# A third product split into quarters, and a reordered value stage, in a cross-attention kernel

## The chip, the core and the metric

The kernel runs on one core of a Trainium2 chip. The metric is the device time of one execution in microseconds (us). Three executions of the kernel before gave 2172.95, 2173.05 and 2175.15 us; the median is 2173.05 us.

## The reference, cut to what matters

The program is a block of three layers on 128 latent tokens of width 512: a double attention (one on the latents themselves, one on a context of 12544 tokens), a causal self-attention, and a mixture of 32 experts. Nearly all of the time goes to the attention on the context:

```python
kvx = jnp.einsum('bsi,oi->bso', cond, w_kv_x)          # 12544 x 512 times 512 x 2048
kx, vx = jnp.split(kvx, 2, axis=-1)
kx = _ln(kx.reshape(b, sc, g, d), kxln_w, kxln_b)      # 8 groups of 128
vx = vx.reshape(b, sc, g, d)
xout = _gqa(qx, kx, vx).reshape(b, s, nh * d)          # 16 heads, two to a group
```

All of it is in fp32.

## The kernel before

**Chunks.** The context is cut into 25 chunks of 512 tokens; the middle one (chunk 12) has 256. For each chunk TensorE makes keys (`KT`, transposed, 8 groups) and values (`V`), then the scores of every group (`s_ps`, function `scores`) and the weighted values (`o_ps`, function `outputs`). Softmax is done with a running maximum: `max_rows` and `spread` find and spread the shift, `weigh` takes the exponential on ScalarE, rescales the running output `ol` by `al`, and adds the probabilities into the running sum on GpSimd.

**Seven products instead of eight.** Keys and values of a chunk are each a product of a 512-wide contraction. It is made as a two by two block product with seven block products (numbered 0 to 6 in the lists `mixed_w` and `mixed`), of sums of the weights (`wsum`, made once) and sums of the tokens (`mix_tokens`, on GpSimd, for each chunk). For whole chunks (`whole(c)`: all but chunk 0 and chunk 12; 23 of them) products 1 and 3 are themselves made from seven quarter products each. That is what `fine` does in `k_chunk` and `v_chunk`, with token sums from `mix_finer_tokens` and weight sums from `mix_finer_weights`. The other five products use `mm`.

**Banks.** All of these products go through the pool `ps_kv` of three PSUM banks. A bank is filled, read by an add on VectorE or a copy on ScalarE, and filled on: several products accumulate in one bank (`a`), and between two of them its contents have to be read. A matmul that writes a bank therefore waits for the reading instruction before it.

**Order of the work.** `v_chunk` is a generator. The loop over the eight groups of a chunk issues `scores(c, g)`, then one step of `v_chunk`, then `maxima`. After the scores, `keys(c + 1, ...)` steps `k_chunk` for the next chunk, and after each step `others(i)` issues `outputs(c, i)`. So the values of chunk c are made between its scores, and the keys of chunk c + 1 between its outputs. The tile framework turns this into one order for each engine, in which an instruction may move a little, and sets the semaphores. Every engine then runs its own list in order.

At the boundary, the last thing in `v_chunk` is product 6 into bank `a`, then two adds on VectorE (L593 and L594). Then `k_chunk` opens three banks:

```python
b, a, d = bank("fb_ps"), bank("fa_ps"), bank("fc_ps")
fine(b, 1, True)
fine(a, 0, True)
p1 = kept(a, "p1", groups)
add(to(0, 0), groups(b), p1)
fine(d, 4, True)
```

`kept` is a copy on ScalarE into a `u` buffer, of which there are two. `fc_ps` gets the bank that L594 reads last.

**Squares of the keys.** `k_sums` squares four groups of keys on ScalarE, 512 columns at a time, into one buffer `sq`, and VectorE reduces each (L603 and L604). `k_rstd` makes the scale `krs` for the scores from them: a small product (`v_ps`), an add on VectorE and a power on GpSimd (L623).

**Buffers.** Probabilities `s` have eight buffers of the pool `sp`, the rescaling tile `al` two.

Of the kernel before, what the change touches and what calls it, by code (L numbers as in the profile page):

```python
# [17 lines left out]
P = 128  # L18
H = 512
# [26 lines left out]
def block_kernel(  # L46
# [359 lines left out]
    def mix_finer_weights(v, eng):  # L406
        s1, s2, s4 = (finer[0][:, v, i] for i in range(3))
        eng.tensor_tensor(s1, finer_w(v, 1, 0), finer_w(v, 1, 1), ALU.add)
        eng.tensor_tensor(s2, s1, finer_w(v, 0, 0), ALU.subtract)
        turn_finer_weights(v, eng)  # L410
        eng.tensor_tensor(s4, finer_w(v, 0, 1), s2, ALU.subtract)

# [9 lines left out]
    def mix_finer_tokens(c, eng):  # L422
        t = finp.tile([P, 2, 3, P], F32, tag="fx", name=f"finer_{c}")
        finer_x[c] = []
        for i, x in enumerate((mixed[c][1], mixed[c][3])):
            b11, b12 = x[:, 0, 0:P], x[:, 0, P : 2 * P]
            b21, b22 = x[:, 1, 0:P], x[:, 1, P : 2 * P]
            t1, t2, t4 = (t[:, i, j, :] for j in range(3))
            eng.tensor_tensor(t1, b12, b11, ALU.subtract)
            eng.tensor_tensor(t2, b22, t1, ALU.subtract)  # L430
            eng.tensor_tensor(b12, b22, b12, ALU.subtract)
            eng.tensor_tensor(t4, b21, t2, ALU.subtract)
            finer_x[c].append((b11, b21, b22, t4, t1, t2, b12))
# [14 lines left out]
    def k_chunk(c):  # L448
# [36 lines left out]
        b, a, d = bank("fb_ps"), bank("fa_ps"), bank("fc_ps")  # L485
# [3 lines left out]
        add(to(0, 0), groups(b), p1)  # L489
        fine(d, 4, True)  # L490
# [15 lines left out]
        d0 = bank("c_ps")  # L506
        mm(d0, 0, 4, True)
        nc.scalar.copy(out(0, 1, 1), pair(d0))
        mm(a0, 0, 5, False)
        u2 = kept(a0, "u2", pair)  # L510
        yield
        mm(d0, 0, 2, False)
        add(out(0, 0, 1), pair(d0), u2)
        mm(a0, 0, 6, False)
        add(out(0, 1, 1), pair(a0), out(0, 1, 1))
        add(out(0, 1, 0), pair(a0), out(0, 1, 0))
        a1 = bank("a_ps")
        mm(a1, 1, 0, True)
        add(out(1, 0, 0), pair(a1), out(1, 0, 0))
        yield  # L520
        d1 = bank("c_ps")
        mm(d1, 1, 4, True)
        nc.scalar.copy(out(1, 1, 1), pair(d1))
        mm(a1, 1, 5, False)
        u2 = kept(a1, "u2", pair)
        yield
        mm(d1, 1, 2, False)
        add(out(1, 0, 1), pair(d1), u2)
        yield
        mm(a1, 1, 6, False)  # L530
        add(out(1, 1, 1), pair(a1), out(1, 1, 1))
        added[0] = add(out(1, 1, 0), pair(a1), out(1, 1, 0))
        yield

    def v_chunk(c):
# [16 lines left out]
        a, b = bank("fa_ps"), bank("fb_ps")  # L552
# [3 lines left out]
        nc.vector.tensor_tensor(to(0, 0), both(b), both(p1), ALU.add)  # L556
# [3 lines left out]
        d = bank("fc_ps")  # L560
# [4 lines left out]
        nc.vector.tensor_tensor(to(1, 1), both(d), both(u3), ALU.add)  # L565
# [4 lines left out]
        nc.vector.tensor_tensor(to(0, 1), both(d), both(u2), ALU.add)  # L570
        yield
        for v in range(2):
            def mm(ps, i, first):
                w, x = mixed_w[i], mixed[c][i]
                for k in range(2):
                    last_mm[0] = nc.tensor.matmul(  # L576
                        ps, lhsT=x[:, k, v * P : (v + 1) * P], rhs=w[:, k, H : 2 * H],
                        start=first and k == 0, stop=k == 1, skip_group_check=True,
                    ).ins

            t1, t2 = V[:, v, :], V[:, 2 + v, :]
            a, d = bank("a_ps"), bank("c_ps")
            mm(a, 0, True)
            nc.vector.tensor_tensor(t1[:, :H], a, t1[:, :H], ALU.add)
            mm(d, 4, True)
            nc.scalar.copy(t2[:, H:], d)
            yield
            mm(a, 5, False)
            u2 = kept(a, "u2")
            mm(d, 2, False)  # L590
            nc.vector.tensor_tensor(t2[:, :H], d, u2, ALU.add)
            mm(a, 6, False)
            nc.vector.tensor_tensor(t2[:, H:], a, t2[:, H:], ALU.add)  # L593
            added[0] = nc.vector.tensor_tensor(t1[:, H:], a, t1[:, H:], ALU.add).ins  # L594
            yield

    def k_sums(c, u):
# [3 lines left out]
        for j in range(4):  # L601
            sq = tmpk.tile([P, CH], F32, tag="sq", name="sq", bufs=1)
            nc.scalar.activation(sq[:, :n], KT[:, 4 * u + j, :n], AF.Square)  # L603
            nc.vector.tensor_reduce(  # L604
                r[:, j, : n // 32], sq[:, :n].rearrange("p (b i) -> p b i", i=32),
                AX.X, ALU.add, apply_transpose=True,
            )
# [26 lines left out]
    def keys(c, others, pool, tag, todo=None, done=0):  # L634
# [4 lines left out]
        for i in range(done, 8):  # L639
            next(todo)  # L640
            if i in ((4, 7) if fine else (3, 7)):
                sums[i // 7] = k_sums(c, i // 7)
            if fine and i == 6:
                k_rstd(c, 0, sums.pop(0), pool, tag)
            if others:
                others(i)
            if fine:
                continue
# [872 lines left out]
```

## Time and profile before

| | us |
|---|---|
| time, three executions | 2172.95, 2173.05, 2175.15 |
| the profiled execution, its own time | 2170.52 |
| its span, first to last instruction | 2168.4 |
| TensorE busy | 2114.5 (98%) |
| VectorE busy | 1441.3 (66%) |
| ScalarE busy | 919.8 (42%) |
| GpSimd busy | 1185.6 (55%) |
| one whole chunk, from its first score product to that of the next | 76.77 |

The last row is read from the timeline of TensorE: the first score products of two following chunks start at 1151.37 and 1228.14. The other whole chunks have the same period within 0.02 us, apart from chunk 11, in front of the short one, and the last. In the profile PE is TensorE, PEld its weight loads, DVE VectorE, ACT ScalarE and POOL GpSimd. One fp32 matmul of the program is two MATMUL records. A timeline row gives the start, the length, the engine, the line, what was written from what, the shape and the number of records, and then the idle time before it with what ended it.

### The profile page before, as it was taken

To read this page: it belongs to the slowest core of one execution; us is meant where nothing else is said; L and a number is where in the kernel's file an instruction comes from. 1 tells how busy PE (TensorE), PEld (TensorE's weight loads), DVE (VectorE), ACT (ScalarE), POOL (GpSimd) and SP (SyncE) were. 2 spreads that over 40 slices of the span, in tenths; PEclk is the share of its full clock that TensorE was granted. 3 is DMA by queue.
4 is the path that set the end of the run, shared out by engine and by line. 5 is a ranking of instruction groups with operands and counts; after the bars stand their busy time and mean duration, and the time that the engine had idled before them with its cause. 6 is when DMAs were issued, how large, how long until landed. Compare 5 with 4: busy or idle time off the path is not lost.

```text
span 2168.4 us, 25820 instructions
## 1 busy us (share of the span) xinstructions
PE 2114.5 (98%) x9487; PEld 1582.4 (73%) x9487; DVE 1441.3 (66%) x2571; ACT 919.8 (42%) x1787; POOL 1185.6 (55%) x1363
## 2 busy tenths in 40 slices
PE   8999999999999999999999999999999999999999
PEld 3667877877877787787777877777787787776554
DVE  8776677677667667766777668667767766766311
ACT  3445444444535434444444445444544443541211
POOL 5245675575566557548675575566557557644000
PEclk9999999999999999999999999999999999999999
DMA  9300000000000000000000000000000000007693
GB/s 320 112 20 1 20 20 1 20 20 20 1 20 20 0 21 20 10 1 20 21 20 12 9 20 20 1 20 20 1 20 20 20 1 20 1 1 258 212 283 115
DMA packets 71230, 95.60 MB, mean 44 GB/s; under 512 B 3136, under 2 KB 39488, under 8 KB 71104
## 3 DMA queue, kind: packets, MB, share of 16 engines
q1 hardware_dynamic: 70816, 93.92, 13.4%
q8 instruction: 74, 1.21, 0.2%
q14 instruction: 52, 0.43, 0.1%
q10 hardware_dynamic: 288, 0.04, 0.0%
HBM read 93.69 MB, written 0.26 MB: 43 GB/s over the span
## 4 chain that ended last, share of the span: by engine, by line
PE 84%; DVE 9%; issue 3%; ACT 2%; POOL 1%; DMA 1%; SPq 0%; POOLq 0%; ACTq 0%; DVEq 0%
PE s_ps L925 15%; PE o_ps L1031 14%; PE a_ps L464 11%; PE a_ps L576 8%; PE c_ps L464 7%; PE c_ps L576 6%; PE gu_ps L1436 4%; PE fa_ps L541 4%; PE fa_ps L455 3%; PE fc_ps L455 2%; PE moe_acc L1457 2%; PE fc_ps L541 2%; DVE mx L953 2%; PE ps_p L722 1%; DVE mxr L936 1%
## 5 line engine op out<-in xcount | busy, mean ns | idle before, releaser
L1023 POOL TENSOR_TENSOR ol<-ol,s 128x256 f32<-128x256 f32 x764 | 550.8, 729 | 55.1 <-ACT s L1013 11.8
L1031 PE MATMUL o_ps<-s,V 128*128 128x256 f32 x1568 | 380.6, 381 | 0.9 <-DVE ol L1036 0.9
L1015 POOL TENSOR_TENSOR ol<-ol,al 128x512 f32<-128x512 f32 x192 | 242.4, 1278 | 241.1 <-DVE al L985 241.1
L930 ACT ACTIVATE s<-s_ps,krs 128x256 f32<-128x256 f32 x784 | 322.5, 472 | 119.8 <-PE s_ps L925 90.1
L925 PE MATMUL s_ps<-qxT,KT 128*128 128x256 f32 x1568 | 372.8, 381 | 0.4 <-ACT s L930 0.4
L623 POOL TENSOR_TENSOR krs<-kve,mhalf 128x16 f32<-128x16 f32 (+1 forms) x50 | 142.8, 2855 | 400.0 <-DVE kve L621 400.0
L936 DVE TRANSPOSE_TENSOR_REDUCE mxr<-s 128x32 f32<-128x1024 f32 (+1 forms) x200 | 244.2, 1221 | 162.3 <-ACT s L930 161.5
L925 PEld LDWEIGHTS s_ps<-qxT,KT 128*128 128x128 f32 x1568 | 295.8, 190 | 72.8 <-issue 35.6
L1031 PEld LDWEIGHTS o_ps<-s,V 128*128 128x128 f32 x1568 | 288.1, 190 | 36.4 <-ACT s L1013 1.3
L603 ACT ACTIVATE sq<-KT 128x512 f32<-128x512 f32 (+1 forms) x200 | 124.1, 621 | 309.1 <-DVE KT L483 216.4
L1013 ACT ACTIVATE s<-s 128x1024 f32<-128x1024 f32 (+1 forms) x200 | 201.3, 1040 | 80.3 <-DVE s L1001 80.2
L1001 DVE TENSOR_TENSOR s<-s,b_ps 128x1024 f32<-128x1024 f32 (+1 forms) x200 | 232.8, 1175 | 0.0
L1036 DVE TENSOR_TENSOR ol<-ol,o_ps 128x256 f32<-128x256 f32 x192 | 79.3, 414 | 203.1 <-PE o_ps L1031 198.4
L604 DVE TRANSPOSE_TENSOR_REDUCE sqr<-sq 128x16 f32<-128x512 f32 (+1 forms) x200 | 139.4, 697 | 72.2 <-ACT sq L603 69.4
L576 PE MATMUL a_ps<-wkv,ctx 128*128 128x512 f32 x368 | 172.9, 592 | 0.0
L464 PE MATMUL a_ps<-ctx,wkv 128*128 128x256 f32 x736 | 170.8, 380 | 0.0
L464 PEld LDWEIGHTS a_ps<-ctx,wkv 128*128 128x128 f32 x736 | 138.0, 190 | 21.4 <-DVE KT L483 3.5
L576 PEld LDWEIGHTS a_ps<-wkv,ctx 128*128 128x128 f32 x368 | 69.9, 190 | 68.4 <-issue 66.0
L445 ACT COPY u<-fa_ps 128x512 f32<-128x512 f32 x92 | 54.0, 587 | 145.2 <-PE fa_ps L455 144.2
L977 ACT ACTIVATE als<-als 128x32 f32<-128x32 f32 x48 | 11.0, 229 | 198.7 <-DVE als L976 198.7
L483 DVE TENSOR_TENSOR KT<-a_ps,KT 128x512 f32<-128x512 f32 x138 | 89.2, 673 | 6.3 <-PE a_ps L464 5.6
L1436 PE MATMUL gu_ps<-gu,xT 128*128 128x384 f32 x256 | 87.4, 486 | 0.0
(319 smaller groups left out, 3243.7 us busy)
## 6 DMA issues: line engine op xcount, KB each, us to landing
ctx<-in_ctxT SPq DMA_DIRECT2D x23, 1024.0 KB, 5.1
gu<-in_w SPq DMA_DIRECT2D x32, 384.0 KB, 4.9
gu<-in_v SPq DMA_DIRECT2D x32, 384.0 KB, 5.6
dn<-in_w SPq DMA_DIRECT2D x16, 768.0 KB, 4.9
w<-in_wprojT SPq DMA_DIRECT2D x8, 1024.0 KB, 5.8
w<-in_wqxT SPq DMA_DIRECT2D x4, 1024.0 KB, 11.3
w<-in_wqT SPq DMA_DIRECT2D x4, 1024.0 KB, 5.5
wkv<-in_wkvT SPq DMA_DIRECT2D x8, 256.0 KB, 8.2
```

What stands on the lines that cost most here:

```text
L464: nc.tensor.matmul(ps[:, j * h : (j + 1) * h], lhsT=w[:, k, (2 * u + j) * D : (2 * u + j + 1) * D], rhs=x[:, k, :], start=first and j == k ...
L576: last_mm[0] = nc.tensor.matmul(ps, lhsT=x[:, k, v * P : (v + 1) * P], rhs=w[:, k, H : 2 * H], start=first and k == 0, stop=k == 1, skip_g ...
L623: nc.gpsimd.tensor_tensor(rs[:, :, :nt], ve[:, :, :nt], mhalf.rearrange("p (g t) -> p g t", g=4)[:, :, :nt], ALU.pow,)
L925: end = nc.tensor.matmul(ps[:, t - t0, :], lhsT=KT[:, g, t * P : (t + 1) * P], rhs=qxT[:, 2 * g : 2 * g + 2, :], start=True, stop=True,)
L930: copied[0] = nc.scalar.activation(s[:, t, :], ps[:, t - t0, :], AF.Copy, scale=rs[:, t : t + 1]).ins
L936: nc.vector.tensor_reduce(mxr[g // 4][:, g % 4, :nt, :].rearrange("p t k -> p (t k)"), s[:, :nt, :].rearrange("p t (k i) -> p (t k) i", i=32),
L1001: nc.vector.tensor_tensor(s[:, :nt, :], s[:, :nt, :], ps[:, a, None, :].to_broadcast([P, nt, HS]), ALU.subtract,)
L1013: nc.scalar.activation(s[:, :nt, :], s[:, :nt, :], AF.Exp, scale=scale)
L1015: nc.gpsimd.tensor_tensor(ol[g], ol[g], rescale[j][:, a, None, :].to_broadcast([P, 2, HS]), ALU.mult)
L1023: summed[0] = nc.gpsimd.tensor_tensor(ol[g][:, 1, :], first, s[:, t, :], ALU.add).ins
L1031: end = nc.tensor.matmul(ps, lhsT=V[:, t, g * D : (g + 1) * D], rhs=s[:, t, :], start=t == 0, stop=t == nt - 1,)
L1436: nc.tensor.matmul(ps, lhsT=xT[:, k, :], rhs=experts[x][0][i][:, k], start=k == 0, stop=k == NK - 1,)
```

## The change

Four things:

- In `v_chunk`, product 2 is made from seven quarter products as well (`third`): seven matmuls of 256 columns take the place of the four of 512 columns that made product 2 for both halves. Their weight sums come from `mix_finer_weights(1, ...)` once, their token sums from `mix_third_tokens` for each chunk, both on GpSimd. Five partial results pass through a bank `t_ps`, whose two halves are filled in turn, and a bank `tb_ps`. The copies `u2` of the two `mm` halves are gone; VectorE adds bank `a` directly.
- In `k_chunk` a `yield` comes after the first two quarter products, so that all of `outputs(c, 0)` stands between them and the third one (`fc_ps`). The later steps are merged so that there are still eight.
- `k_sums` squares two groups at a time (1024 columns) and takes its buffer from the pool `sp` of the probabilities.
- `al` has one buffer, and is filled after the subtraction of the shift instead of before it. `mx4` has one buffer too. For j = 2 of a whole chunk the spreading of the shift is held back until the last add of `v_chunk`.

```diff
@@ mix_finer_weights
+        if v:
+            s1, s2, s4 = (finer[1][:, i] for i in range(3))
+            eng.tensor_tensor(s1, third_w(1, 0), third_w(1, 1), ALU.add)
+            eng.tensor_tensor(s2, s1, third_w(0, 0), ALU.subtract)
+            turn_third_weights(eng)
+            eng.tensor_tensor(s4, third_w(0, 1), s2, ALU.subtract)
...
+    def mix_third_tokens(c, eng):
+        t = finp.tile([P, 3, P], F32, tag="tx", name=f"third_{c}")
+        third_x[c] = mix_tiles(t, mixed[c][2], eng)
@@ k_chunk
-        b, a, d = bank("fb_ps"), bank("fa_ps"), bank("fc_ps")
+        b, d, a = bank("fb_ps"), bank("fc_ps"), bank("fa_ps")
         fine(b, 1, True)
         fine(a, 0, True)
         p1 = kept(a, "p1", groups)
         add(to(0, 0), groups(b), p1)
+        yield
         fine(d, 4, True)
@@ v_chunk
+        def third(ps, n, first, start=None):
+            nc.tensor.matmul(
+                ps, lhsT=tx[n], rhs=tw[n], start=first if start is None else start, stop=True,
+                skip_group_check=True,
+            )
...
+        y = bank("tb_ps")
+        third(y[:, : H // 2], 1, True)
...
+        t = bank("t_ps")
+        ta, td = t[:, : H // 2], t[:, H // 2 :]
+        third(ta, 0, True)
+        p1 = kept_half(ta, "p1")
+        add(third_to(0, 0), y[:, : H // 2], p1)
+        a = bank("a_ps")
+        mm(a, 0, 0, True)
+        add(outs(0)[0], a)
+        third(td, 4, True, False)
+        third(ta, 5, False)
+        u2 = kept_half(ta, "u2")
+        yield
+        third(ta, 6, False)
+        u3 = kept_half(ta, "u3")
+        add(third_to(1, 1), td, u3)
+        d = bank("c_ps")
+        mm(d, 0, 4, True)
+        nc.scalar.copy(outs(0)[3], d)
+        third(ta, 3, False)
+        nc.scalar.copy(third_to(1, 0), ta)
+        mm(a, 0, 5, False)
+        third(td, 2, False)
+        add(third_to(0, 1), td, u2)
+        add(outs(0)[2], d)
+        add(outs(0)[2], a)
+        yield
+        mm(a, 0, 6, False)
+        add(outs(0)[3], a)
+        add(outs(0)[1], a)
+        a = bank("a_ps")
+        mm(a, 1, 0, True)
+        add(outs(1)[0], a)
+        yield
+        d = bank("c_ps")
+        mm(a, 1, 5, False)
+        add(outs(1)[2], a)
+        mm(d, 1, 4, True)
+        nc.scalar.copy(outs(1)[3], d)
+        add(outs(1)[2], d)
+        mm(a, 1, 6, False)
+        add(outs(1)[3], a)
+        added[0] = add(outs(1)[1], a)
@@ k_sums
-        for j in range(4):
-            sq = tmpk.tile([P, CH], F32, tag="sq", name="sq", bufs=1)
+        for j in range(0, 4, 2):
+            sq = pool.tile([P, CH // P, HS], F32, tag="s", name="sq", **({} if c else {"bufs": 1}))
...
@@ spread
-        to_all(ps, sh)
-        if c:
-            rescale[j] = tmp.tile([P, 2, HS], F32, tag="al", name="al")
-            to_all(rescale[j], al)
+        with tc.issue_after(added[0]) if whole(c) and j == 2 else nullcontext():
+            to_all(ps, sh)
         for a in range(2):
...
+        if c:
+            rescale[j] = tmp.tile([P, 2, HS], F32, tag="al", name="al", bufs=1)
+            with tc.issue_after(end.ins):
+                to_all(rescale[j], al)
@@ loop over the groups
+            if g == 0 and whole(c):
+                mix_third_tokens(c, nc.gpsimd)
```

## The prediction

> **What bounds the kernel now.** I read the page's busy shares first, then the waits of TensorE, then the timeline of one whole chunk.
>
> ```profile
> PE 2114.5 (98%) x9487; PEld 1582.4 (73%) x9487; DVE 1441.3 (66%) x2571; ACT 919.8 (42%) x1787; POOL 1185.6 (55%) x1363
> ```
>
> TensorE is the bound: 54 us of its span are idle. Its waits say where.
>
> ```profile
> PE fc_ps L455 <- DVE V L594: 28.7, 21, 1.4
> PE ps_t L252 <- DVE xn L215: 6.0, 1, 6.0
> PE fc_ps L455 <- DVE KT L483: 2.4, 2, 1.7
> ```
>
> One wait recurs, at 21 chunk boundaries: the first `fc_ps` product of the next keys wants the bank that the last add of the values (L594) still reads. In the timeline of TensorE:
>
> ```profile
> 1153.10 0.59 PE L541 MATMUL fa_ps<-wkv,ctx 128*128 128x256 f32 x2
> 1153.53 0.59 PE L541 MATMUL fa_ps<-wkv,mix 128*128 128x256 f32 x2
> ...
> 1168.15 1.88 PE L576 MATMUL c_ps<-wsum,mix 128*128 128x512 f32 x4
> 1169.87 1.89 PE L925 MATMUL s_ps<-qxT,KT 128*128 128x256 f32 x8
> ...
> 1190.57 0.60 PE L1031 MATMUL o_ps<-s,V 128*128 128x256 f32 x2
> 1192.53 1.13 PE L455 MATMUL fc_ps<-finer,finer 128*128 128x128 f32 x8 [1.36 <-DVE V L594]
> 1193.49 1.06 PE L455 MATMUL fa_ps<-finer,finer 128*128 128x128 f32 x8
> ```
>
> Start to start, a matmul of 256 columns (two records) takes 0.43 us and one of 512 columns 0.86 us (1.72 for two). The `o_ps` pair started at 1190.57 is through at 1191.00, so the wait costs 1.53 us, and the product behind it 0.07 more than its usual 0.89. All else in the 76.77 us of a chunk is back to back. Why L594 is late stands in the timeline of VectorE:
>
> ```profile
> 1164.06 1.25 DVE L936 TRANSPOSE_TENSOR_REDUCE mxr<-s 128x32 f32<-128x1024 f32 x1 [0.77 <-ACT s L930]
> 1165.23 0.65 DVE L570 TENSOR_TENSOR V<-fc_ps,u 128x512 f32<-128x512 f32 x1
> 1165.80 1.49 DVE L953 TENSOR_REDUCE mx<-mxr 32x32 f32<-32x128 f32 x4
> 1167.32 1.50 DVE L963 TENSOR_REDUCE m_new<-mx 32x32 f32<-32x128 f32 x4
> 1168.86 1.25 DVE L936 TRANSPOSE_TENSOR_REDUCE mxr<-s 128x32 f32<-128x1024 f32 x1
> ...
> 1184.71 1.25 DVE L936 TRANSPOSE_TENSOR_REDUCE mxr<-s 128x32 f32<-128x1024 f32 x1 [1.47 <-ACT s L930]
> ...
> 1191.12 0.67 DVE L593 TENSOR_TENSOR V<-a_ps,V 128x512 f32<-128x512 f32 x1
> 1191.71 0.67 DVE L594 TENSOR_TENSOR V<-a_ps,V 128x512 f32<-128x512 f32 x1
> ```
>
> And in the busy times by stretch:
>
> ```profile
> 1164.10:1192.50 28.40, 27.07 (x94) 16.20 (x93) 26.16 (x48) 13.86 (x28) 19.78 (x28) 1.00 0.07 21
> 1192.50:1228.10 35.60, 35.57 (x190) 31.53 (x191) 20.18 (x32) 11.79 (x18) 24.42 (x25) 1.00 0.04 15
> ```
>
> The columns are length, PE, PEld, DVE, ACT and POOL. Over the 66% of the page lies a stretch of 28 us in which VectorE is 92% busy. The value stage stands in it.
>
> **The change part by part.** Times t count from the chunk's first score product (1151.37 in the trace). The order of the instructions, and which instruction each wait is for, are those of the built program.
>
> *TensorE's own work.* Four matmuls of 0.858 go, seven of 0.432 come: 3.43 - 3.02 = -0.41 us a chunk. A rule speaks against this: the Trainium skill, "TensorE: Matmul & The Clock Gate", section "Back-to-back issue gap", gives a sustained stream of weight load and matmul 81 ns at 128 columns and 131 at 512, so small matmuls cost far more for each column. Interpolated, 256 columns would be about 98: seven against four is then 686 to 524, and the split would cost 3.43 x 0.31 = +1.06 us a chunk, which puts the whole sum at about 2204. I take the rows: 256 columns follow each other at half of 512 here, with the weight load of 190 ns inside the 216 of a record.
>
> *The boundary.* All four `o_ps` matmuls (1.73) instead of one now stand before `fc_ps`. Whether L594's successor is in time must be walked.
>
> *VectorE's list* has per chunk two more adds of 512 columns (0.58 start to start) and three of 256 (0.33, from L1036): +2.15 us, all in the full stretch. A second rule would make it dearer: "VectorE: DVE Perf Modes", section "The DRAIN you can't avoid", has the next operation start only when the pipe is empty, that is after the whole duration. Over the walk below that adds up to about 1.0 us a chunk, 23 in all. The rows start the follower of a 0.65 add 0.58 later, and of 1.25 maxima 1.17 later; I take those.
>
> The walk starts where VectorE last idles, at the maxima of the fourth group. `tb_ps` stands before its scores (+0.43), so it starts at 13.12 (before: 12.69). Then: maxima 1.17, add 0.58, L953's four 1.52, L963's four 1.54, maxima 1.17, half add 0.34, add 0.58, four small ones 0.66, two spreads 0.63 and 0.59, subtraction 1.13, maxima 1.17, half add of `u3` 0.34: 24.5. The quarter product 3 into `t_ps` waits for that half add, since it writes the same bank. From the add's start plus 0.42 and 0.15 (as L594 to `fc_ps`) TensorE may go at 24.74. It is there at 23.26, from adding up its list. **New wait: 1.48, plus 0.07.** Queued behind it on TensorE is everything; nobody waits for VectorE meanwhile.
>
> Further: product 6 of the first half waits for the second add into `V[2]`; allowed at 28.26, wanted at 28.26. Product 6 of the second half waits for an add behind the maxima of the eighth group; these wait for ScalarE, which has an exponential between the score copies: allowed at 37.30, wanted at 37.08: **0.22, plus 0.07.** `fa_ps` has 0.4 to spare. `fc_ps` is wanted at 42.4 and allowed at 42.1: the old wait is gone. The next two waits for VectorE in `k_chunk` have 0.2 each to spare.
>
> *Per chunk:* -0.41 - 1.60 + 1.55 + 0.29 = -0.17 us, times 21 = -3.6.
>
> *Ends.* Chunk 11 has no old wait to lose: +1.4. The last chunk has none either; its V adds end late, L963's successor starts 1.7 later, and the fifth output, held by the exponential, starts at 46.4 against 45.4; with GpSimd's later sums I take +1.2. At chunk 12 to 13 the 1.7 wait (second `fc_ps`) gets half a product in front of it: about -1.5. Together +1.1.
>
> *Hidden.* Squares: eight of 0.63 on ScalarE become four of about 1.0 (L1013's shape), eight reductions of 0.70 become four of 1.22 (L936's shape). Both lie where VectorE is 57% busy. Their buffer is free: GpSimd has added up those probabilities at t = 43, the squares come at 62. The eighth group's buffer, which the next chunk's fourth group now takes, is free at 63, wanted at 88. Scale `krs`: `v_ps` comes at t = 71, the power of 2.9 ends at 74.8, ScalarE wants it at 77.7; losing that cover would delay the first scores. GpSimd's four token operations (0.41 each) lie in its idle time before the first `al`. This `al` is 6 us later (27 against 21), but GpSimd's idle 3.1 and 1.5 us further on take that up: its sums end at 63 (before 61), the mixing at 68, `krs` wants it at 72. One `al` buffer: refilled at 33.4 and 50.8, free at 29.7 and 49.6. The four weight operations of chunk 0 (about 2.8 us) fall into GpSimd's idle 4.9 before its first sums. No DMA, and nothing in SP's queue, moves.
>
> Sum: 2170.5 - 3.6 + 1.1 = 2168.0 for the profiled execution. The median of the runs is 2.5 higher than that execution: **2170.5**.
>
> **The rivals.**
> *Forecast, 0.52: the wait moves from the boundary into the third product.* Each allowed time is a sum of some ten durations, so I give the balance of a chunk +-0.3 us, +-7 in all. Most of that is no measurable change.
>
> *Faster, 0.22: VectorE gets to the half add of `u3` sooner than summed.* For it: ScalarE's copy, the true reason for that wait, could let it go early, and the boundary's 1.6 us go in any case. Against: thirteen rows make the sum. With half of the 1.55 gone: 23 x 0.78 = 18 less, 2153.
>
> *Slower, 0.22: VectorE sets the pace of the whole value stage.* Its cover behind the new wait is thin: 0.0 at product 6, 0.2 to 0.3 at three later waits. If its thirteen instructions up to the `u3` add cost their full durations instead of what lies start to start (0.07 to 0.1 more each), `t_ps` waits 1.0 longer: 23 us, 2194; at half of that 2182. It decides from a lag of 0.2 us on, 4.6 in all; from 0.3 on the three later waits join. Against: the pitches are of the same instructions.
>
> *Nothing but the order takes effect, 0.04:* the boundary is covered, the third product costs what it saves: 2139.
>
> **How the numbers follow.** Three executions differ by 2.2 us, 0.1%; 0.2% is 4.3 us, about what a measurement of this kernel can tell from no change. The forecast's share splits 0.30 below 2168.7, 0.62 within, 0.08 above 2177.4. Faster: 0.16, 0.17 of the faster rival and the 0.04, together 0.37; within: 0.32 and the other 0.05, 0.37; slower: 0.04 and 0.22, 0.26. Range: 2154 to 2186, which leaves out the far halves of both rivals and the last case, about 0.2; the forecast alone 2164 to 2177.
>
> **What would show it.** The old wait `fc_ps` for V should vanish from TensorE's waits, and `t_ps` waiting for V come with 23 times about 1.3 to 1.4 us (the idle column counts 0.17 less than start to start), `a_ps` for V with about 0.2. The period should be 76.6. A `t_ps` wait under 0.8 us makes the faster rival right; further waits of `a_ps` or `fc_ps` for VectorE above 0.5 us the slower one; `s_ps` or ScalarE waiting for `krs` would mean that GpSimd's cover was misjudged.

## The result, and the profile after

| | before | after |
|---|---|---|
| median of the executions (us) | 2174.1 (4, 2172.95 to 2175.51) | 2205.51 (4, 2198.91 to 2206.11) |
| ratio, 95% interval | | 1.0137 (1.0116 to 1.0158) |
| the profiled execution, its span (us) | 2170.52, 2168.4 | 2206.03, 2204.2 |
| one whole chunk (us) | 76.77 | 77.62 |

The change makes the kernel 1.4% slower; the forecast was 2170.5, in a range up to 2186. The two spans differ by 35.8 us. Reading the first score product of every chunk in both timelines shows where: 21 whole chunks at +0.85 are 17.9; chunk 0 is +1.2, chunk 11 is +1.4, the step from chunk 12 to 13 is +7.8, and all behind the last chunk's first score is +7.6 (all rounded).

The busy shares of the page after:

```profile
PE 2129.1 (97%) x9625; PEld 1617.8 (73%) x9625; DVE 1494.8 (68%) x2590; ACT 920.6 (42%) x1733; POOL 1206.8 (55%) x1461
```

TensorE has less work in each chunk, yet its busy time is up by 14.6 us. Part of that is records at half clock, shown further down: stretches in which the profile gives TensorE a granted clock of 0.50 and its records follow each other at twice the usual distance. The waits of TensorE (who waited for whom, then the total, how often, and the longest):

```profile
PE t_ps L573 <- DVE V L595: 27.0, 23, 1.2
PE a_ps L487 <- DVE KT L506: 18.3, 22, 0.9
...
PE a_ps L388 <- ACT p L339: 3.0, 1, 3.0
```

The old wait of `fc_ps` for the values is gone, as forecast. `t_ps` waits 23 times, as forecast. The second line was not forecast: the first `a_ps` product of the keys waits for the add into `KT` at nearly every boundary. In TensorE's timeline of one chunk, which starts at 1171.16:

```profile
1193.55 1.02 PE L589 MATMUL a_ps<-wsum,mix 128*128 128x512 f32 x2
1195.74 0.70 PE L573 MATMUL t_ps<-wsum,third 128*128 128x256 f32 x2 [1.17 <-DVE V L595]
1196.28 1.02 PE L589 MATMUL a_ps<-wsum,mix 128*128 128x512 f32 x2
...
1211.59 1.89 PE L1107 MATMUL o_ps<-s,V 128*128 128x256 f32 x8
1213.32 1.05 PE L478 MATMUL fc_ps<-finer,finer 128*128 128x128 f32 x8
1214.21 1.06 PE L478 MATMUL fa_ps<-finer,finer 128*128 128x128 f32 x8
1216.10 1.99 PE L487 MATMUL a_ps<-ctx,wkv 128*128 128x256 f32 x8 [0.83 <-DVE KT L506]
```

The records of this chunk, added up from start to start, can be set against the usual pitch of each shape (the usual time from one start to the next). The work goes from 74.49 to 74.08, and about 0.6 around the two `v_ps` products is the same in both. The other terms are the old wait and its tail (what the record behind a wait takes more than usual) -1.60, the `t_ps` wait +1.44, the `a_ps` wait +1.10 (1.00, and 0.10 more for the product behind it), two smaller waits +0.21 (last product 6 of the values) and +0.16 (second `fc_ps`). The sum is -0.41 - 1.60 + 1.44 + 1.10 + 0.37 = +0.90, against +0.85 measured.

Why the add into `KT` is late stands in the timeline of VectorE:

```profile
1210.21 1.50 DVE L1036 TENSOR_REDUCE m_new<-mx 32x32 f32<-32x128 f32 x4
1211.74 1.29 DVE L595 TENSOR_TENSOR V<-a_ps,V 128x512 f32<-128x512 f32 x2
1212.95 1.31 DVE L1041 TENSOR_TENSOR m_new<-m_new,qb 128x32 f32<-128x32 f32 x1
1214.30 0.19 DVE L1043 TENSOR_TENSOR m_new<-m_new 128x32 f32<-128x32 f32 x1
...
1214.75 0.73 DVE L1058 STREAM_TRANSPOSE b_ps<-sh 128x512 f32<-128x512 f32 x1
1215.38 0.67 DVE L506 TENSOR_TENSOR KT<-fb_ps,p 128x512 f32<-128x512 f32 x1
```

and in that of GpSimd over the same stretch:

```profile
1206.22 2.52 POOL L1091 TENSOR_TENSOR ol<-ol,al 128x512 f32<-128x512 f32 x2
1208.67 5.54 POOL L1099 TENSOR_TENSOR ol<-ol,s 128x256 f32<-128x256 f32 x8
1219.33 2.52 POOL L1091 TENSOR_TENSOR ol<-ol,al 128x512 f32<-128x512 f32 x2 [5.11 <-DVE al L1058]
```

L1041, from here on the small add, is an add of 32 columns that reads two SBUF operands; with the three behind it, it makes the four small instructions. The small add takes 1.31 us here, 0.17 in the same chunk's first maxima round, and 0.19 at this place before the change. The row does not count this as idle time: the instruction has started, and is not finished. It ends at 1214.26, 0.05 us after the last of GpSimd's eight sums (1214.21). Before the change, VectorE and GpSimd at the same place:

```profile
1189.81 0.19 DVE L968 TENSOR_TENSOR m_new<-m_new,qb 128x32 f32<-128x32 f32 x1
1181.40 8.55 POOL L1023 TENSOR_TENSOR ol<-ol,s 128x256 f32<-128x256 f32 x11
```

GpSimd's run of sums ended at 1189.95 and the small add began at 1189.81: it missed the run but for its last 0.14 us.

### The profile page after: what moved, and what is told of

Read it like the earlier page. It is cut to its first block, busy times and chain, and to the rows that moved or that the text cites. A ratio compares the mean times of both kernels' runs of the same rounds, so it can differ in the third digit from the quotient of the medians.

```text
span 2204.2 us, 26440 instructions
## 1 busy us (share of the span) xinstructions
PE 2129.1 (97%) x9625; PEld 1617.8 (73%) x9625; DVE 1494.8 (68%) x2590; ACT 920.6 (42%) x1733; POOL 1206.8 (55%) x1461
## 4 chain that ended last, share of the span: by engine, by line
PE 69%; DVE 20%; issue 4%; ACT 3%; POOL 3%; DMA 1%; SPq 0%; POOLq 0%; DVEq 0%; ACTq 0%
PE o_ps L1107 12%; PE a_ps L487 11%; PE s_ps L998 10%; PE c_ps L487 7%; PE a_ps L589 6%; DVE V L595 4%; DVE mxr L1009 4%; PE gu_ps L1515 4%; PE fa_ps L555 3%; DVE m_new L1036 2%; ACT s L1003 2%; DVE mx L1026 2%; PE fa_ps L478 2%; PE moe_acc L1536 2%; DVE b_ps L1058 2%
## 5 line engine op out<-in xcount | busy, mean ns | idle before, releaser
L1099 POOL TENSOR_TENSOR ol<-ol,s 128x256 f32<-128x256 f32 x764 | 530.2, 736 | 1.3
L1107 PE MATMUL o_ps<-s,V 128*128 128x256 f32 x1568 | 371.9, 379 | 2.1 <-ACT s L1089 1.4
L1089 ACT ACTIVATE s<-s 128x1024 f32<-128x1024 f32 (+1 forms) x200 | 206.1, 1039 | 58.0 <-DVE s L1073 57.4
L675 ACT ACTIVATE sq<-KT 128x1024 f32<-128x1024 f32 (+1 forms) x100 | 103.8, 1040 | 237.1 <-DVE KT L506 157.4
L679 DVE TRANSPOSE_TENSOR_REDUCE sqr<-sq 128x32 f32<-128x1024 f32 (+1 forms) x104 | 121.0, 1168 | 4.1 <-ACT sq L675 4.1
L595 DVE TENSOR_TENSOR V<-a_ps,V 128x512 f32<-128x512 f32 x184 | 119.9, 671 | 0.7
L446 POOL TENSOR_TENSOR third<-ctx 128x128 f32<-128x128 f32 x23 | 10.5, 457 | 185.9 <-PE t_ps L573 185.9
L589 PE MATMUL a_ps<-wsum,mix 128*128 128x512 f32 x184 | 90.2, 592 | 0.0
```

The lines of the kernel that those rows point to most:

```text
L589: last_mm[0] = nc.tensor.matmul(ps, lhsT=x[:, k, v * P : (v + 1) * P], rhs=w[:, k, H : 2 * H], start=first and k == 0, stop=k == 1, skip_g ...
L595: return nc.vector.tensor_tensor(o, a, o if b is None else b, ALU.add).ins
L1089: nc.scalar.activation(s[:, :nt, :], s[:, :nt, :], AF.Exp, scale=scale)
L1099: summed[0] = nc.gpsimd.tensor_tensor(ol[g][:, 1, :], first, s[:, t, :], ALU.add).ins
L1107: end = nc.tensor.matmul(ps, lhsT=V[:, t, g * D : (g + 1) * D], rhs=s[:, t, :], start=t == 0, stop=t == nt - 1,)
```

## The experiments

Theory A: VectorE's instructions with two SBUF operands and GpSimd's get in each other's way, and the change moved GpSimd's sums to where the small add comes. Theory B: the small add is slow for a reason of its own, or the wait has nothing to do with it.

**GpSimd held while the small instructions run.**

```diff
@@ weigh
                 summed[0] = nc.gpsimd.tensor_tensor(ol[g][:, 1, :], first, s[:, t, :], ALU.add).ins
+                if whole(c) and g == 3 and t >= 2:
+                    held.append(summed[0])
@@ max_rows, behind the last of the four small instructions (al)
+            if j0 == 2:
+                for i in held:
+                    tc.add_manual_dep(
+                        i, last.name,
+                        mybir.DependencyInfo(mybir.DependencyClass.Sync, mybir.DependencyReason.DATA),
+                        reason="held",
+                    )
```

> The changed kernel, but the last two GpSimd sums of the fourth group wait until the four small VectorE instructions of the second maxima round are done, so that GpSimd is idle while these run. Order of every other engine unchanged. Theory A (VectorE and GpSimd get in each other's way at SBUF): the small add m_new<-m_new,qb, which takes 1.31 us in each chunk of the changed kernel, falls to about 0.17 to 0.19; the a_ps wait for the add into KT (0.83 idle, 1.10 start to start) goes; period 77.62 - 1.10 = 76.5; time about 2205.5 - 23 = 2182. Theory B (the small add is slow for a reason of its own, such as what stands in front of it on VectorE): it stays at 1.31 us, the period at 77.6 and the time at 2205.

Measured: 2177.97 us (10 executions), ratio to before 1.0022 (1.0013 to 1.0031), 27.5 less than the changed kernel; the period is 76.50. VectorE's timeline at the small add:

```profile
1198.15 0.18 DVE L1041 TENSOR_TENSOR m_new<-m_new,qb 128x32 f32<-128x32 f32 x1
```

and GpSimd's around it:

```profile
1193.87 4.29 POOL L1107 TENSOR_TENSOR ol<-ol,s 128x256 f32<-128x256 f32 x6
1198.97 1.53 POOL L1107 TENSOR_TENSOR ol<-ol,s 128x256 f32<-128x256 f32 x2 [0.81 <-DVE als L1049]
```

The order of VectorE and TensorE was not changed. The small add is back at 0.18, and the `a_ps` wait is gone. Theory A holds, and this alone is most of the loss.

**The add into KT ahead of the small instructions.**

```diff
@@ max_rows
-        nc.vector.tensor_tensor(m, m, q, ALU.add)
+        with tc.issue_after(opened[0]) if j0 == 2 and c + 1 < NCH and whole(c + 1) else nullcontext():
+            nc.vector.tensor_tensor(m, m, q, ALU.add)
```

(`opened[0]` is the add into `KT` from `fb_ps`.)

> The changed kernel, but on VectorE the add KT<-fb_ps is issued ahead of the four small instructions of the second maxima round instead of behind them and the spread after them. Both theories (A: the small add is held up by GpSimd; B: it is slow of itself) expect the a_ps wait to go and about 2182, since the wait is then no longer behind the slow instruction. Under A the small add starts 0.6 later and takes about 0.7 instead of 1.31, because it ends when GpSimd's last sum ends, as in the changed kernel; under B it still takes 1.31. If the wait is not for that add's place at all but for ScalarE's copy or a bank, the time stays at 2205.

Measured: 2189.1 us, ratio 1.007 (1.0057 to 1.0083), period 76.85. VectorE's timeline at the boundary:

```profile
1206.24 0.68 DVE L506 TENSOR_TENSOR KT<-fb_ps,p 128x512 f32<-128x512 f32 x1
1206.83 0.71 DVE L1042 TENSOR_TENSOR m_new<-m_new,qb 128x32 f32<-128x32 f32 x1
```

The small add takes 0.71, as A expected: starting 0.6 later, it ends at the same point of GpSimd's run. The `a_ps` wait is gone. Only 16 of the expected 23 us came back, 0.77 of the 1.10 in each chunk: the rest of VectorE's list is still late, and the second `fc_ps` now waits 0.47 with its tail where it waited 0.16. Chunk 0 is 1.5 longer as well: both kernels have a pause of 2.4 us there, and in this one it was followed by 3.4 us at half clock, in the changed kernel not.

**The third product undone.** `v_chunk` as it was before the change, all else as changed.

```diff
@@ v_chunk
-        y = bank("tb_ps")
-        third(y[:, : H // 2], 1, True)
...
@@ loop over the groups
-            if g == 0 and whole(c):
-                mix_third_tokens(c, nc.gpsimd)
```

> The changed kernel with product 2 of the values made by four matmuls of 512 columns again (values as before the change), all else as changed: first output between the first key products, squares in pairs, rescaling tile filled late. Forecast's view: the old wait of 1.60 at 21 boundaries is gone, nothing takes its place, so 2173 - 34 + 2 = about 2141. Theory A adds that GpSimd's sums still end late (about t = 42 of a chunk), while the small add comes earlier than in the changed kernel (about t = 39), so it should take 0.7 to 2 us; the add into KT behind it has about 2 us to spare, so the time is 2141 to 2160. If the late rescaling tile or the squares cost more than was seen, it is above 2165.

Measured: 2213.61 us, ratio 1.0188 (1.0174 to 1.0203). This is slower than with the third product. The expectation had 2141 to 2160, or above 2165 if the late tile or the squares cost more than was seen; that taking the third product out would cost time, nothing had said. VectorE's timeline:

```profile
1213.95 2.77 DVE L979 TENSOR_TENSOR m_new<-m_new,qb 128x32 f32<-128x32 f32 x1
```

GpSimd's:

```profile
1211.16 5.51 POOL L1037 TENSOR_TENSOR ol<-ol,s 128x256 f32<-128x256 f32 x8
```

and TensorE's:

```profile
1218.62 2.05 PE L472 MATMUL fc_ps<-finer,finer 128*128 128x128 f32 x8 [2.03 <-DVE V L602]
```

Without the third product's adds VectorE gets to the small add 1.5 us earlier in GpSimd's run, so it is held 2.77 us, over four sums, to the run's end (1216.67). Here the last adds of the values stand behind it, and the next keys' `fc_ps` waits for them in spite of the output in between. Behind that wait come records of 128 columns at 213 ns instead of 112 after 13 of the 21 boundaries between two whole chunks: those chunks have a period of 79.05, the other eight one of 77.50. That is half clock, 1.55 us of it.

**The yield undone.** The keys stepped as before the change; the third product, squares and rescaling tile as changed.

```diff
@@ k_chunk
         add(to(0, 0), groups(b), p1)
-        yield
         fine(d, 4, True)
```

> The changed kernel with the keys stepped as before the change (third quarter product in front of the first output), the third value product, the squares and the rescaling tile as changed. The last add of the values is read at about t = 41.9, and fc_ps would be wanted at about 40.9, so a wait of 1.0 to 1.5 us comes back there; the a_ps wait, wanted that much later, shrinks by as much. So about the same as the changed kernel, 2200 to 2215; if the yield is what made the change slow, it falls to about 2180.

Measured: 2226.66 us, ratio 1.0244 (1.023 to 1.0259), period 78.76. The waits of TensorE:

```profile
PE t_ps L582 <- DVE V L604: 27.0, 23, 1.2
PE fc_ps L478 <- DVE V L604: 20.8, 21, 1.0
PE a_ps L487 <- DVE KT L506: 19.2, 22, 0.9
```

The boundary wait returns (1.22 with its tail), and the `a_ps` wait does not shrink: 1.22 of waiting stand where 1.30 of output stood, so that `a_ps` is wanted no later. So the yield is worth 1.14 us a chunk, and the time is above the 2200 to 2215 that were expected. It was not what made the change slow.

**The third product undone, GpSimd held.** The edits of the first and the third experiment together.

> Third product undone as in the run before it, and in addition the last two GpSimd sums of the fourth group wait for the four small VectorE instructions, so that GpSimd stands still while these run. Theory A: the small add took 2.77 us without this and falls to about 0.18, the add L602 is read 2.6 us earlier, and the fc_ps wait (2.19 start to start, 0.07 behind it, and sometimes 1.55 for half clock after it) goes: period 79.05 and 77.50 both to about 75.2, time about 2174 - 21 x 1.55 = 2141. If the wait has another cause, it stays at about 2213.

Measured: 2161.6 us, ratio 0.9947 (0.9933 to 0.996), period 76.02. Better than before the change, but not the 75.2 that was expected. Only two of the eight sums are held, and VectorE now gets to its small instructions while the other six still run: the first takes 0.71 us and the second 0.76, and `fc_ps` waits 0.77 with its tail. Each of the two ends 0.05 after a sum behind which GpSimd's run has a gap: 0.08 behind the fifth sum, which the sixth has to wait for, and 0.46 behind the sixth. The four sums before had none. The direction was right, the size was not.

**The rescaling tile filled early**, with everything else as changed, the third product included.

```diff
@@ spread
+        if c:
+            rescale[j] = tmp.tile([P, 2, HS], F32, tag="al", name="al", bufs=1)
+            to_all(rescale[j], al)
         for a in range(2):
...
-        if c:
-            rescale[j] = tmp.tile([P, 2, HS], F32, tag="al", name="al", bufs=1)
-            with tc.issue_after(end.ins):
-                to_all(rescale[j], al)
```

> The changed kernel with the rescaling tile filled ahead of the subtraction of the shift, as before the change (one buffer still). Theory A': the late rescaling tile is what makes GpSimd's sums run into the small instructions. Then GpSimd's run ends some 2 to 4 us earlier in the chunk, the small add takes about 0.2, the a_ps wait goes (-1.10), and the t_ps wait grows by the 0.6 of one more spread ahead of it: 77.1 a chunk, about 2195. If GpSimd is late because of the third product's token operations, which wait for the last t_ps, the small add still takes about 1.3 and the time is 2205 to 2220.

Measured: 2173.6 us (13 executions), ratio 1.0003 (0.9994 to 1.0011), period 76.45: the whole loss is gone by the place of two lines. The `t_ps` wait stayed at 1.17 idle, since the order put the one spread more where the other had been, so the expected +0.6 did not come. GpSimd's timeline:

```profile
1189.43 6.25 POOL L1098 TENSOR_TENSOR ol<-ol,s 128x256 f32<-128x256 f32 x8
```

and VectorE's:

```profile
1194.69 0.22 DVE L1041 TENSOR_TENSOR m_new<-m_new,qb 128x32 f32<-128x32 f32 x1
```

This does not go the way the expectation's theory A' had it. GpSimd is still in its run of sums (to 1195.68) when the small add comes, and the small add takes only 0.22. The sums themselves differ: 6.25 us for eight, not 5.54. With the tile early, GpSimd adds the four tiles of one group and then those of the other, each sum of a group waiting for the one before, with a gap of about 0.08 between. With the tile late, the two groups' sums alternate, every 0.685, with no gap.

**Sums in turn.** That difference alone, on the changed kernel.

```diff
@@ weigh
-                summed[0] = nc.gpsimd.tensor_tensor(ol[g][:, 1, :], first, s[:, t, :], ALU.add).ins
+                with tc.issue_after(summed[0]) if whole(c) and j == 1 and (a or t) else nullcontext():
+                    summed[0] = nc.gpsimd.tensor_tensor(ol[g][:, 1, :], first, s[:, t, :], ALU.add).ins
```

> The changed kernel, but GpSimd adds the four probability tiles of the third group one after the other and then those of the fourth, where the changed kernel alternates between the two. The same eight sums; now each reads what the one before it wrote, which elsewhere in these traces gives one every 0.78 to 0.80 us with a gap of about 0.08, against every 0.685 with no gap. Order of all other engines unchanged, and GpSimd still busy when VectorE gets to the small add. Theory A1 (VectorE gets in only at a gap between GpSimd instructions, and alternating sums leave none): the small add waits at most for the sum in progress, 0.2 to 0.8 us instead of 1.31, the a_ps wait of 1.10 shrinks to at most 0.5, and the time is 2180 to 2192. Theory A2 (VectorE waits until GpSimd has nothing more queued): GpSimd ends 0.8 us later, the small add takes about 2.1 us, the time is about 2222.

Measured: 2196.89 us, ratio 1.0107 (1.0093 to 1.0121), period 77.12 in most chunks. GpSimd's timeline:

```profile
1206.09 6.30 POOL L1100 TENSOR_TENSOR ol<-ol,s 128x256 f32<-128x256 f32 x8
```

and VectorE's:

```profile
1210.37 0.40 DVE L1041 TENSOR_TENSOR m_new<-m_new,qb 128x32 f32<-128x32 f32 x1
1210.81 0.19 DVE L1043 TENSOR_TENSOR m_new<-m_new 128x32 f32<-128x32 f32 x1
1211.04 0.60 DVE L1045 TENSOR_TENSOR sh<-m_new,qb 128x32 f32<-128x32 f32 x1
```

A1 holds in the whole chunks and A2 falls: with gaps in the run the small add waits for the sum in progress only (0.40 instead of 1.31), though GpSimd works on for 1.6 us more. Another of the four is now caught (0.60), so the `a_ps` wait is 0.60 with its tail, and the time is some 5 us above the range given.

**The late rescaling tile alone, on the kernel before.** The edit of the sixth experiment the other way round, with two buffers.

```diff
@@ spread
-        if c:
-            rescale[j] = tmp.tile([P, 2, HS], F32, tag="al", name="al")
-            to_all(rescale[j], al)
         for a in range(2):
...
+        if c:
+            rescale[j] = tmp.tile([P, 2, HS], F32, tag="al", name="al")
+            with tc.issue_after(end.ins):
+                to_all(rescale[j], al)
```

> The kernel before the change with one part of the change alone: the rescaling tile (two buffers, as before) filled after the subtraction. If the late tile alone makes the collision, GpSimd's two chains of sums alternate and run until about t = 41.3 of a chunk, the small add, which VectorE reaches at about t = 38.4, takes 2.5 to 2.8 us instead of 0.19, the last add L594 is later by as much, and the fc_ps wait grows from 1.5 to about 4.1: about 2174 + 21 x 2.6 = 2229, more where TensorE then runs at half clock for a while. If the third product's work is needed for the collision, it stays at 2174.

Measured: 2286.93 us, ratio 1.0524 (1.051 to 1.0539), period 81.9. VectorE's timeline:

```profile
1248.36 2.78 DVE L968 TENSOR_TENSOR m_new<-m_new,qb 128x32 f32<-128x32 f32 x1
```

TensorE's:

```profile
1253.67 2.04 PE L455 MATMUL fc_ps<-finer,finer 128*128 128x128 f32 x8 [3.96 <-DVE V L594]
1255.51 1.92 PE L455 MATMUL fa_ps<-finer,finer 128*128 128x128 f32 x8
1257.21 1.06 PE L464 MATMUL a_ps<-ctx,wkv 128*128 128x256 f32 x2
```

and the busy times by stretch (length, then PE, PEld, DVE, ACT and POOL, then the granted clock):

```profile
1250.00:1255.00 5.00, 1.33 (x6) 1.36 (x7) 4.93 (x9) 0.70 (x2) 1.09 (x2) 0.71 0.47 178
1255.00:1260.00 5.00, 5.00 (x21) 4.52 (x20) 3.82 (x5) 0.59 (x1) 2.50 (x2) 0.61 0.00 0
```

The small add, held 2.78 us, is within the forecast. The time is 58 us above the 2229 given, which named half clock without a price. This part of the change, alone, costs 113 us. Of the 5.1 us in each chunk 2.6 are the longer wait; the other 2.5 go with the clock, 0.71 and 0.61 in and behind the 4 us pause.

**Only the order.** Values as before, rescaling tile early with two buffers; what stays of the change is the yield, the squares in pairs, the held-back spread and the one `mx4` buffer.

```diff
@@ spread, on the kernel with the third product undone
+        if c:
+            rescale[j] = tmp.tile([P, 2, HS], F32, tag="al", name="al")
+            to_all(rescale[j], al)
         for a in range(2):
...
-        if c:
-            rescale[j] = tmp.tile([P, 2, HS], F32, tag="al", name="al", bufs=1)
-            with tc.issue_after(end.ins):
-                to_all(rescale[j], al)
```

> Only the first output between the keys' first products, the squares in pairs and the held-back spread of the third pair of groups: values as before the change, rescaling tile with two buffers and filled ahead of the subtraction. The prediction's case that nothing but the order takes effect: 2139. Theory A says the same, if GpSimd's run ends before the small add as it does before the change (it ended 0.05 us before that add there): then the fc_ps wait of 1.60 is gone and the period is 75.2. If the small add now meets GpSimd (it comes up to 0.5 us earlier), it is longer by up to 0.7 us, which the output in between covers. Chunk 12 to 13, where one rescaling buffer cost VectorE two idle stretches of 0.86, should return to about 54 from 57 to 62.

Measured: 2137.78 us, ratio 0.9838 (0.9824 to 0.9851), period 75.13, chunk 12 to 13 in 55.31 (about 54 was expected). It beats both kernels. The small add takes 0.19, GpSimd's run ends at 1172.72 while it runs, and the timeline of TensorE shows no gap at the boundary:

```profile
1173.36 1.89 PE L1043 MATMUL o_ps<-s,V 128*128 128x256 f32 x8
1175.09 1.05 PE L472 MATMUL fc_ps<-finer,finer 128*128 128x128 f32 x8
1175.98 1.06 PE L472 MATMUL fa_ps<-finer,finer 128*128 128x128 f32 x8
1176.87 1.89 PE L481 MATMUL a_ps<-ctx,wkv 128*128 128x256 f32 x8
```

Against the kernel with the tile early and the third product (period 76.45) it also prices that product in a whole chunk: -0.41 of work, +1.44 for `t_ps`, +0.30 for the first key products, +1.33 together. The 35.8 us between the two kernels are not the product's alone, since they differ in the number of `al` buffers too.

**The squares one at a time again**, on the order-only kernel.

```diff
@@ k_sums
-        for j in range(0, 4, 2):
+        for j in range(4):
+            sq = tmpk.tile([P, CH], F32, tag="sq", name="sq", bufs=1)
+            nc.scalar.activation(sq[:, :n], KT[:, 4 * u + j, :n], AF.Square)
```

> The order-only kernel with the squares of the keys one group at a time in a buffer of their own, as before the change. The prediction put the squares at nothing, since they lie beside work of TensorE that is longer: the same time as the order-only kernel, 2138 within 3. If the squares in pairs were worth something (or cost something), it shows here as a difference of more than 4 us.

Measured: 2140.62 us, ratio 0.9848 (0.9835 to 0.9862), the same period of 75.13. The 2.8 us lie in the step from chunk 12 to 13 (57.18 against 55.31) and behind the last chunk. Squares in pairs are hidden, as forecast.

**VectorE relieved in the value stage.** On the changed kernel the spread and subtraction of the second pair of groups come after the last add of the values, and the half add of `u3` goes ahead of the second subtraction and the sixth maxima.

```diff
@@ maxima
+        if whole(c) and i == 6:
+            return
+        if whole(c) and i == 8:
+            spread(c, 1)
+            weigh(c, 1)
@@ spread
-        with tc.issue_after(added[0]) if whole(c) and j == 2 else nullcontext():
+        with tc.issue_after(added[0]) if whole(c) and j in (1, 2) else nullcontext():
...
+            with tc.issue_after(half[0]) if whole(c) and j == 0 and a else nullcontext():
...
@@ v_chunk
-        add(third_to(1, 1), td, u3)
+        half[0] = add(third_to(1, 1), td, u3)
+        tc.add_manual_dep(
+            maxi[0], half[0].name,
...
```

> The changed kernel with VectorE's work of the value stage put off where nothing waits for it: the spread and subtraction for the second pair of groups come after the last add of the values, and the half add of u3 is issued ahead of the second subtraction and of the maxima of the sixth group. The forecast's reason for the t_ps wait (that half add stands behind maxima and a subtraction): the wait, 1.44 with what follows it, falls to under 0.2, and GpSimd's sums for the second pair begin after the small instructions, so the a_ps wait (1.10) goes as well: period 77.62 - 2.5 = about 75.1, about 2152. If t_ps waits for ScalarE's copy of u3, it stays above 1.0 and the time is about 2180; if GpSimd becomes late for krs, s_ps waits for ScalarE and the time is above 2180.

Measured: 2288.01 us, ratio 1.0531 (1.0514 to 1.0549), a miss. The waits of TensorE:

```profile
PE a_ps L487 <- DVE KT L506: 69.9, 22, 4.4
PE t_ps L573 <- DVE V L595: 15.2, 23, 0.7
```

The `t_ps` wait fell to 0.66, not under 0.2, and 3.5 us of VectorE's work now stand in the key stage in front of adds that `a_ps` wants: a wait of 3.2 us in each chunk there, and half clock behind it in about half of the chunks (periods of 81.2 and 79.5). That VectorE's queue sets the `t_ps` wait is borne out; that the key stage has room for what is put off is not.

## Why the prediction was wrong

*TensorE's work, -0.41.* Right to the hundredth. The page's rule for small matmuls ("TensorE: Matmul & The Clock Gate", "Back-to-back issue gap"), which would have made it +1.06, does not hold for these records: 256 columns still follow at 216 ns, 512 at 429. That the sum with that rule, about 2204, lies beside the measured 2205.51 is chance.

*The boundary, -1.60.* Right: the wait is gone from the list. The order-only kernel brings exactly this (76.77 to 75.13).

*The new `t_ps` wait, +1.55.* Right: +1.44, 23 times. The half add of `u3` started at t = 24.14, and TensorE could go at 24.58 against 24.74 forecast. The pitches held: full durations would have made the wait about 1.0 longer.

*Product 6, +0.29.* Right in size: +0.21.

*"The next two waits in `k_chunk` have 0.2 each to spare."* This is the step that failed. The first of them cost 1.10, the second 0.16. The list of VectorE up to the add into `KT` was right in order and in number; the small add in it was counted at its pitch of 0.22 and took 1.35. Over the 21 chunks that is 23 of the 35 us between forecast and result. With GpSimd held, the small add is at 0.18 and the period at 76.50, against 76.6 forecast.

*GpSimd, "hidden".* The cause lay in view. The prediction had `al` 6 us later (27 against 21; it came at 26.3 to 27.0) and followed who waits for GpSimd. It did not ask what GpSimd shares with VectorE while it runs. The Trainium skill states it: "SBUF — State Buffer", "SBUF: two separate sides", has VectorE and GpSimd share a pair of ports, which a GpSimd instruction and a VectorE instruction with two SBUF inputs take for a whole instruction, the other one blocked. The trace agrees in kind: of VectorE's instructions in the whole chunks of the changed kernel only this one is longer under GpSimd's work. The adds that read PSUM and SBUF (`V<-a_ps,V`: 0.67 alone and 0.68 beside GpSimd) and the reductions are not. In size it differs: the rule holds one instruction long, at most 0.75 us here, while the small add was held over two sums (1.31) and over four (2.78).

*One `al` buffer, "free in time".* Right for whole chunks. In chunk 12, where the work is halved, VectorE stood idle twice for 0.86 until GpSimd let go of it.

*Chunk 0, nothing.* Wrong: +1.2. The weight operations were set against GpSimd's idle time before its first sums, but the power for `krs` stands in between: with the third product's weight and token operations in front it starts at 137.84 instead of 134.51, ScalarE waits 3.51 us for it, and TensorE 2.44 for ScalarE. With the third product undone chunk 0 is 60.9, as before the change.

*Chunk 11, +1.4.* Measured as forecast.

*Chunk 12 to 13, -1.5.* Wrong: +7.8. ScalarE waited 6.78 us for `krs`, which GpSimd reached late, where it had waited 3.08, and TensorE 2.96 for ScalarE. ScalarE's timeline after the change, and before it:

```profile
1038.39 0.84 ACT L1003 ACTIVATE s<-s_ps,krs 128x256 f32<-128x256 f32 x2 [6.78 <-POOL krs L698]
1024.68 0.84 ACT L930 ACTIVATE s<-s_ps,krs 128x256 f32<-128x256 f32 x2 [3.08 <-POOL krs L623]
```

After its pause TensorE ran at half clock. Its timeline:

```profile
1039.76 3.78 PE L388 MATMUL a_ps<-wsum,mix 128*128 128x512 f32 x4 [2.96 <-ACT p L339]
```

and the busy times by stretch, columns as above:

```profile
1030.00:1035.00 5.00, 5.00 (x19) 3.28 (x18) 2.10 (x6) 1.15 (x2) 4.84 (x6) 1.00 0.00 2
1035.00:1040.00 5.00, 2.04 (x8) 1.11 (x7) 0.73 (x2) 1.61 (x5) 4.51 (x6) 0.89 0.00 0
1040.00:1045.00 5.00, 5.00 (x6) 1.95 (x7) 1.20 (x2) 1.04 (x3) 0.00 (x0) 0.50 0.00 0
```

Seven records of 512 columns came about every 0.85 instead of 0.43: 2.95 us. The rest is the longer wait and four waits of 0.9 to 1.4 in the next keys, three of them for VectorE, where there was one of 1.8. "`krs` is late" was named as the sign of a misjudged GpSimd, but looked for in the whole chunks only, where it did not come. It takes the third product's work and the late tile together: the step takes 62.1 with both, 57.3 with the tile early, 57.2 with the third product undone, and 55.3 with neither and a second `al` buffer, against 54.3 before the change.

*The last chunk, +1.2.* The attention on the context ends 2.0 later, near the forecast. The other 5.6 of the 7.6 come behind it, where both kernels run the same instructions, and where the profile after has 10 us at a granted clock of 0.50 to 0.55, which would make about 5 of them. Whether an execution meets such a stretch varies: the one of the four at a mean clock of 0.999 took 2198.91, those at 0.995 and 0.996 took 2204.98 to 2206.11.

*The rivals.* The slower one gave the right sign to look for (an `a_ps` wait above 0.5), but for another reason: the instructions keep their pitches, one of them collides. "Nothing but the order" was put at 2139 and given 4 in 100; built for itself it is 2137.78. The chances were wrong because the balance of a chunk was given +-0.3 us on the strength of durations that were all taken where GpSimd's run lay elsewhere.

## What to carry to other kernels

When a change moves one engine's work in time, look not only for who waits for it, but for what runs on the engine that shares its memory port at the new place, and take no duration across such a move. A tiny VectorE instruction with two SBUF operands in a queue that the bound engine waits for is such a place: keep GpSimd's runs of independent instructions away from it, or make them depend on each other so that there are gaps (which gave back 8.6 us here, where holding two sums back gave 27.5). And a pause of TensorE of about 2 us can bring half clock behind it, which cost 1.5 to 3 us each time here, so that waits of that size are to be priced higher than their length.

## What was not expected of the hardware

- A VectorE add of 128x32 with two SBUF operands took 0.17 to 0.19 us alone. Beside GpSimd sums that followed each other every 0.685 us without a gap it took 0.71, 1.31 or 2.77 to 2.78, as it met the last one, two or four of them, and 0.22 to 0.76 where the sum beside it had a gap of 0.08 or more behind it. In the first case it ended 0.05 us after the end of the whole run, in the second 0.05 us after the end of that one sum.
- This is not all: in chunk 12 of the changed kernel the four small instructions took 0.30, 0.65, 0.65 and 0.76, each ending behind one GpSimd instruction of a run without gaps. What lets VectorE in there was not settled.
- TensorE's granted clock fell to 0.50 after pauses of 2.96 us (chunk 12), 3.96 us (the kernel with the late tile alone), and 2.02 to 2.06 us (13 of 21 times in the kernel with the third product undone). After the 21 pauses of about 1.36 us of the kernel before it never did; after one of 1.88 us (chunk 12 of the order-only kernel with the old squares) it did. The Trainium skill has the gate look at windows of about 3.4 us that run freely, and throttle after an idle one ("TensorE: Matmul & The Clock Gate", Part 1). The trace agrees in the length: from the first chunk to the last, every stretch at half clock in these runs lasts 3.41 or 6.83 us. Windows that run freely also fit a 2 us pause meeting it only at times. But these pauses are shorter than a window, so how much of one has to be idle is not shown.
